# A four-layer graph network on one core: giving each tile the buffer that the plan chose for it

## The chip, the core and the metric

The kernel runs on one core of a Trainium2 chip. A core has TensorE (PE, matrix products and transposes into PSUM), VectorE (DVE), ScalarE (ACT), GpSimd (POOL) and SyncE (SP), which here only issues DMA transfers. Each engine runs its own instructions in the order in which the program gives them. The metric is the time of one execution on the device in microseconds; smaller is better.

## The reference, cut to what matters

There are 64 independent graphs of 256 nodes with 256 features, all in float32. Four graph layers follow each other, each with its own residual and layer norm:

```python
# x, adj: (64, 256, 256)
x = _layernorm(x + L0(x, adj))   # 4 heads: sigmoid(q k^T) * adj, scaled by degree^-1/2 on both sides, times X; layer norm
x = _layernorm(x + L1(x, adj))   # 8 heads: softmax(q k^T where adj > 0), times v, then W_o
x = _layernorm(x + L2(x, adj))   # (adj + eps) x, W1 (256 to 1024), rms norm, silu, W2
x = _layernorm(x + L3(x, adj))   # one-head attention from two scores, softmax, times Wh, layer norm, gelu
```

## The kernel before

**Tiling.** A graph has two blocks of 128 nodes, and a feature axis two blocks of 128. Nearly every tile is 128 partitions by 512 words: both blocks side by side. The function `graph` describes the work of one graph as a list of `Op`s. An Op has an engine, an estimated cost, a function that issues its instructions, and the tiles (`Value`s) that it writes and reads. Nothing is issued while the list is made.

**The order.** `Plan.order` goes through all 64 graphs' Ops at once with a small model of the engines' clocks. Again and again it takes the ready Op that can start soonest, and among equals the one due first. Graphs so overlap: while one is in its last layer, others are in earlier ones. The order that comes out is kept: the framework is told not to reorder (`manual_schedule`), and each engine runs its list front to back. An instruction that must wait holds all that stand behind it on the same engine. Before an ACT function whose table isn't loaded, the build places a table load.

**The buffers.** There are six kinds of tile, each with a fixed number of buffers:

```python
WORDS = {"s": 516, "d": 1024, "b": 2048, "c": 32, "p": 512, "h": 1024}
SLOTS = {"s": 42, "d": 10, "b": 3, "c": 72, "p": 8, "h": 8}
```

Kind `s` is the 512-word tile in SBUF, `p` a bank of PSUM, `c` a few scalars per partition, `h` a scratch area in DRAM. The model also keeps the buffers' books: when a tile is first needed it takes the slot that the model says falls free earliest (`v.slot = self.free[v.kind].pop(0)[1]`), and gives it back at the modelled end of the last use. In the kernel before, `v.slot` serves this reckoning alone. `emit` asks the framework's pool of that kind for a tile, and the pool itself decides which of its 42 (10, 3, ...) buffers that is. The framework adds the waits: the first writer of a tile waits until all who use the buffer's former tile are done.

**The steps that are named below**, by line and by the name of their output in the profile:

- Layer 0: L502 (PE, attention scores), L506 (ACT, sigmoid, `att`), L508 (DVE, times adjacency), L514 (DVE, `added`, sums two halves of `att`), L520 (PE, sums `added` over nodes), L542 (PE, reads `v` and `att`), L553 (DVE).
- Layer 1: L582 (PE, scores), L465 and L470 (DVE and ACT, softmax), L618 (PE, attention times `v1` into `av`), L628 and L631 (SP, the softmax sums out to DRAM and back as `rb`), L635 (DVE, `yT` = `av` times `rb`), then PE's product of `yT` with `w_o` at L379.
- Layer 2: L649 and L661 (PE), L666 and L668 (ACT, squares and `hT`), L673 and L675 (DVE, sums of squares), L680 (PE), L697 (DVE), L699 (ACT, silu), L707 (PE).
- Layer 3: L722 (PE), L731 (PE), L335, L341 and L345 (DVE and SP, a transpose by way of DRAM, giving `xT` and `eT`), L453 and L456 (DVE, `y`), L746 (ACT, gelu in place on `y`).
- Everywhere: L323 (PE transposes), L359 (ACT, copies out of PSUM), L368 and L379 (PE, products with weights), L436 (DVE, `y` = product plus residual), L393, L395, L405, L406 and L416 (DVE and POOL, mean and deviation), L420 (ACT, the normalized tile `x`), L431 (DVE, residual plus a row, `xb`).

Of the kernel before, what the change touches and what calls it, by code (L numbers as in the profile page):

```python
# [9 lines left out]
F32 = mybir.dt.float32  # L10
# [3 lines left out]
P = 128  # L14
# [15 lines left out]
WORDS = {"s": 516, "d": 1024, "b": 2048, "c": 32, "p": 512, "h": 1024}  # L30
# [10 lines left out]
SLOTS = {"s": 42, "d": 10, "b": 3, "c": 72, "p": 8, "h": 8}  # L41
# [710 lines left out]
@with_exitstack  # L752
def gnn_stack_kernel(ctx: ExitStack, tc: tile.TileContext, t: dict, out: bass.AP):

    nc = tc.nc
    x_in, xT_in, adj_in, adjT_in = t["x"], t["xT"], t["adj"], t["adjT"]
    B, N, D = x_in.shape
    NB, DB = N // P, D // P
    assert NB == 2 and DB == 2
    H0, H1 = 4, 8
    HD0, HD1 = D // H0, D // H1
    HID = t["L2_gnn_W1"].shape[1]
    HB = HID // P  # L770

    const = ctx.enter_context(tc.tile_pool(name="const", bufs=1))
    pools = {kind: ctx.enter_context(tc.tile_pool(name=f"pool_{kind}", bufs=SLOTS[kind], **(
        {"space": {"p": bass.MemoryType.PSUM, "h": bass.MemoryType.DRAM}[kind]} if kind in "ph" else {})))
        for kind in SLOTS}


    ident = const.tile([P, P], F32, name="ident")
    make_identity(nc, ident)
    ones = const.tile([P, 32], F32, name="ones")  # L780
    nc.vector.memset(ones, 1.0)
    mean_of = const.tile([P, 32], F32, name="mean_of")
    nc.vector.memset(mean_of, 1.0 / HID)
    mhalf = const.tile([P, 8], F32, name="mhalf")
    nc.vector.memset(mhalf, -0.5)
    c = SimpleNamespace(const=const, ident=ident, ones=ones, mean_of=mean_of, mhalf=mhalf)

    plan = Plan(B)
    weights(plan, nc, c, t)
    for b in range(B):  # L790
        plan.graph = b
        graph(plan, nc, c, t, out, b)
    engines = {mybir.EngineType.PE, mybir.EngineType.DVE, mybir.EngineType.Activation, mybir.EngineType.Pool,
               mybir.EngineType.SP}
    with tc.manual_schedule(engines=engines):
        emit(plan, pools)


def emit(plan, pools):
    for op in plan.order():  # L800
        for v in op.takes:
            v.full = pools[v.kind].tile([P, WORDS[v.kind]], F32, tag=v.kind, name=v.name)
            v.t = v.full[:, :512] if v.kind == "s" else v.full
        op.fn()

# [30 lines left out]
```

## Time and profile before

| | |
|---|---|
| time, median of 3 runs | 2722.47 us (2721.5 to 2724.49) |
| profiled execution, its own time | 2719.01 us |
| its span, first to last instruction | 2717.2 us |
| busy PE, DVE, ACT, POOL | 2669.2, 2438.3, 2231.0, 594.8 us |
| granted TensorE clock | 0.998 of full |
| instructions in the profile | 56606 |

The span is the stretch in which the profile can place work; the 1.8 us between it and the execution's own time lie around it. "Busy" counts the time in which an engine computes, not the time in which it waits. In a list of waits, `A <- B` means that A's engine stood idle before A, and that what came last of the things A needed was B. In the chain of waits, each step is followed back from the last instruction to what released it.

### The profile page before, as it was taken

To read this page: it belongs to the slowest core of one execution; us is meant where nothing else is said; L and a number is where in the kernel's file an instruction comes from. 1 tells how busy PE (TensorE), PEld (TensorE's weight loads), DVE (VectorE), ACT (ScalarE), POOL (GpSimd) and SP (SyncE) were. 2 spreads that over 40 slices of the span, in tenths; PEclk is the share of its full clock that TensorE was granted. 3 is DMA by queue.
4 is the path that set the end of the run, shared out by engine and by line. 5 is a ranking of instruction groups with operands and counts; after the bars stand their busy time and mean duration, and the time that the engine had idled before them with its cause. 6 is when DMAs were issued, how large, how long until landed. Compare 5 with 4: busy or idle time off the path is not lost.

```text
span 2717.2 us, 56606 instructions
## 1 busy us (share of the span) xinstructions
PE 2669.2 (98%) x17568; PEld 2142.3 (79%) x17568; DVE 2438.3 (90%) x7480; ACT 2231.0 (82%) x5343; POOL 594.8 (22%) x902
## 2 busy tenths in 40 slices
PE   8999999999999999999999999999999999999997
PEld 6778787787787877877878777877778788787776
DVE  6888999899899998999989999989999899999986
ACT  4978788887887888878888888888888888888886
POOL 1121222212222222222222222222222222222212
PEclk9999999999999999999999999999999999999999
DMA  5476776776676766767767677676676676766661
GB/s 153 149 205 187 202 205 178 192 205 179 188 193 176 214 186 181 198 172 204 207 161 205 184 189 211 170 190 193 172 215 188 171 212 183 191 210 177 174 169 38
DMA packets 708045, 501.01 MB, mean 184 GB/s; under 512 B 309792, under 2 KB 667552, under 8 KB 707744
## 3 DMA queue, kind: packets, MB, share of 16 engines
q1 hardware_dynamic: 707744, 497.40, 66.5%
q8 instruction: 140, 2.29, 0.4%
q14 instruction: 161, 1.32, 0.2%
HBM read 301.35 MB, written 195.82 MB: 183 GB/s over the span
## 4 chain that ended last, share of the span: by engine, by line
PE 87%; DVE 5%; ACT 3%; DMA 3%; SPq 1%; issue 1%; POOL 0%; DVEq 0%; ACTq 0%; POOLq 0%
PE ps L368 16%; PE ps L379 15%; PE ps L707 14%; PE ps L661 14%; PE ps L582 4%; PE ps L542 4%; PE ps L502 4%; PE ps L722 4%; PE ps L649 4%; PE av L618 4%; DMA eT<-far 1%; PE ps L323 1%; PE ps L520 1%; DVE st L393 1%; ACT e L470 1%
## 5 line engine op out<-in xcount | busy, mean ns | idle before, releaser
L470 ACT ACTIVATE e<-e,low 128x256 f32<-128x256 f32 x1152 | 574.8, 500 | 84.3 <-DVE low L465 83.5
L707 PE MATMUL ps<-w,hT 128*128 128x256 f32 x2048 | 466.8, 380 | 1.3 <-ACT hT L699 1.2
L661 PE MATMUL ps<-aggT,w 128*128 128x256 f32 x2048 | 463.4, 380 | 1.6 <-ACT aggT L359 1.0
L707 PEld LDWEIGHTS ps<-w,hT 128*128 128x128 f32 x2048 | 385.7, 190 | 60.4 <-issue 4.6
L661 PEld LDWEIGHTS ps<-aggT,w 128*128 128x128 f32 x2048 | 383.3, 190 | 57.0 <-issue 2.8
L405 POOL TENSOR_SCALAR mv<-mv 128x2 f32<-128x2 f32 x384 | 132.9, 346 | 1348.3 <-DVE mv L395 966.7
L465 DVE CUSTOM_DVE_ANT_0 e<-ps,adj 128x256 f32<-128x256 f32 x1024 | 361.7, 419 | 25.2 <-PE ps L582 25.1
L406 POOL TENSOR_TENSOR mv<-mv,mhalf 128x2 f32<-128x2 f32 x384 | 307.6, 801 | 32.0
L603 DVE STREAM_TRANSPOSE eb<-e 128x1024 f32<-128x1024 f32 x248 | 301.1, 1222 | 0.8 <-ACT e L470 0.7
L668 ACT ACTIVATE hT<-ps,br,r 128x256 f32<-128x256 f32 x512 | 255.6, 584 | 35.1 <-PE ps L707 31.8
L420 ACT ACTIVATE x<-y,mv 128x256 f32<-128x256 f32 x384 | 215.2, 599 | 55.4 <-DVE mv L416 51.8
L666 ACT ACTIVATE sq<-ps,b 128x256 f32<-128x256 f32 x512 | 219.8, 473 | 27.2 <-PE ps L661 25.0
L393 DVE BATCH_NORM_STATS2 st<-y 128x6 f32<-128x256 f32 x640 | 238.9, 410 | 1.2
L470 ACT ACTIVATION_READ_ACCUMULATOR e<-e,low 128x1 f32 x1152 | 219.4, 190 | 0.0
L508 DVE TENSOR_TENSOR att<-att,adjT 128x512 f32<-128x512 f32 x256 | 166.8, 677 | 7.9 <-ACT att L506 7.9
L688 POOL TENSOR_TENSOR rs<-rs,mhalf 128x2 f32<-128x2 f32 x64 | 45.6, 712 | 526.7 <-DVE rs L686 521.2
L528 POOL TENSOR_TENSOR dp<-dp,mhalf 128x8 f32<-128x8 f32 x64 | 109.7, 1714 | 210.3 <-DVE dp L527 164.4
L697 DVE TENSOR_TENSOR hT<-hT,pr 128x1024 f32<-128x1024 f32 x128 | 150.0, 1210 | 5.2 <-PE pr L693 4.5
L582 PE MATMUL ps<-kT,qT 32*128 32x256 f32 x2048 | 147.5, 400 | 0.0
L673 DVE TENSOR_TENSOR sq<-sq 128x512 f32<-128x512 f32 x192 | 129.9, 677 | 12.1 <-ACT sq L666 11.1
L368 PE MATMUL ps<-x0T,w_q 128*128 128x256 f32 x512 | 130.0, 384 | 6.1 <-DMA x0T<-in_xT 6.1
L506 ACT ACTIVATE att<-ps 128x512 f32<-128x512 f32 x256 | 132.2, 603 | 3.9 <-PE ps L502 3.2
(119 smaller groups left out, 5511.4 us busy)
## 6 DMA issues: line engine op xcount, KB each, us to landing
far<-eb SPq DMA_DIRECT2D x248, 512.0 KB, 3.6
eT<-far SPq DMA_DIRECT2D x992, 128.0 KB, 4.1
adj<-in_adj SPq DMA_DIRECT2D x128, 256.0 KB, 5.0
far<-eb SPq DMA_DIRECT2D x488, 64.0 KB, 2.0
x0T<-in_xT SPq DMA_DIRECT2D x64, 256.0 KB, 4.8
adjT<-in_adjT SPq DMA_DIRECT2D x64, 256.0 KB, 5.0
x<-in_x SPq DMA_DIRECT2D x64, 256.0 KB, 5.2
adj<-in_adjT SPq DMA_DIRECT2D x64, 256.0 KB, 4.6
```

Of the source, the lines that this page charges most:

```text
L368: pe.matmul(two(ps)[:, o, :], w.t[:, k, o * P:(o + 1) * P], two(xT)[:, k, :], start=(k == 0), stop=(k == DB - 1))
L379: pe.matmul(two(ps)[:, n, :], two(xT)[:, k, n * P:(n + 1) * P], w()[:, k, :], start=(k == 0), stop=(k == DB - 1))
L393: op("DVE", 328, lambda n=n: dve.bn_stats(st.t[:, 6 * n:6 * n + 6], two(src)[:, n, :]), [(st, n)], [(src, n)])
L406: pool.tensor_tensor(m()[:, :, 2], m()[:, :, 2], c.mhalf[:, :NB], OP.pow)
L465: op("DVE", 345, lambda n=n: dve.tensor_tensor_reduce(out=E(n), in0=two(logits)[:, n, :], in1=two(negmask)[:, n, :], scale=-scale, scalar= ...
L470: op("ACT", 491, lambda n=n: act.activation(E(n), E(n), AF.Exp, bias=low.t[:, n:n + 1], scale=-1.0, accum_out=r.t[:, col(n):col(n) + 1]), ...
L582: pe.matmul(two(pss[i])[:, n, :], two(qT1)[s, hq, n * P:(n + 1) * P], two(kT1)[s, hq, :], start=True, stop=True)
L603: op("DVE", 1155, lambda e=e, eb=eb: dve.transpose(eb.t.rearrange("p (b g i) -> p g b i", b=4, i=32), e.t.rearrange("p (g b i) -> p g b i" ...
L661: pe.matmul(two(ps)[:, i, :], c.w2_1.t[:, k, (j + i) * P:(j + i + 1) * P], two(aggT)[:, k, :], start=(k == 0), stop=(k == DB - 1))
L666: op("ACT", 357, lambda ps=ps, sq=sq, i=i, j=j: act.activation(two(sq)[:, i, :], two(ps)[:, i, :], AF.Square, bias=c.b2_1.t[:, j + i:j + i ...
L668: op("ACT", 491, lambda ps=ps, i=i, j=j: act.activation(Hb(j + i)[:, 0], two(ps)[:, i, :], AF.Identity, bias=c.br2.t[:, j + i:j + i + 1], ...
L707: pe.matmul(two(ps)[:, n, :], Hb(j)[:, 0, n * P:(n + 1) * P], c.w2_2.t[:, j, :], start=(j == 0), stop=(j == HB - 1))
```

## The change

Each slot gets a pool tag of its own with a single buffer, so `s0`, `s1` and so on up to `h7`. When a tile is taken, the tag is made of its kind and of the slot number that the plan wrote into `v.slot`. So the pool has nothing left to choose: the tile lies where the plan's books say. The numbers of buffers, the sizes, the list of Ops and the plan's model are untouched. The title of the change speaks of "the order in which ACT helps DVE in the last three graphs": that order is set by `ENDS = 3` in `normed` and `affine`, and stands in both kernels.

```diff
-    pools = {kind: ctx.enter_context(tc.tile_pool(name=f"pool_{kind}", bufs=SLOTS[kind], **(
+    pools = {kind: ctx.enter_context(tc.tile_pool(name=f"pool_{kind}", bufs=1, **(
         {"space": {"p": bass.MemoryType.PSUM, "h": bass.MemoryType.DRAM}[kind]} if kind in "ph" else {})))
         for kind in SLOTS}
...
     for op in plan.order():
         for v in op.takes:
-            v.full = pools[v.kind].tile([P, WORDS[v.kind]], F32, tag=v.kind, name=v.name)
+            v.full = pools[v.kind].tile([P, WORDS[v.kind]], F32, tag=f"{v.kind}{v.slot}", name=v.name)
             v.t = v.full[:, :512] if v.kind == "s" else v.full
         op.fn()
```

## The prediction

> **What bounds the kernel now.** I read the page first: shares by engine, then the chain that ended last.
>
> ```profile
> PE 2669.2 (98%) x17568; PEld 2142.3 (79%) x17568; DVE 2438.3 (90%) x7480; ACT 2231.0 (82%) x5343; POOL 594.8 (22%) x902
> ...
> PE 87%; DVE 5%; ACT 3%; DMA 3%; SPq 1%; issue 1%; POOL 0%; DVEq 0%; ACTq 0%; POOLq 0%
> ```
>
> TensorE is busy 98% of 2717.2 us and makes up 87% of the chain. Nothing in the change shortens a matmul, so all that can be won is TensorE's idle time, 2717.2 - 2669.2 = 48 us, of which some belongs to start and end. Next, the waits of PE, from 300 to 2250 us, where the graphs follow each other in a steady pattern:
>
> ```profile
> PE ps L323 <- ACT x L420: 5.6, 10, 1.0
> PE ps L379 <- DVE mv L395: 2.9, 10, 0.4
> PE ps L323 <- DVE y L436: 2.3, 5, 0.5
> PE ps L520 <- DVE added L514: 2.2, 5, 0.4
> ```
>
> The columns are total us, times, longest. All come 5 or 10 times: the pattern repeats every 334 us (eight graphs), five times in this stretch. (The line "mv L395" is really the yT multiply L635, which ends 0.1 us earlier; L379 reads yT.) What are those DVE and ACT results late for? The waits of DVE over the whole span:
>
> ```profile
> DVE y L436 <- PE av L618: 11.2, 9, 1.6
> ...
> DVE added L514 <- PE ps L379: 9.5, 5, 1.9
> DVE yT L635 <- PE ps L542: 9.1, 7, 1.6
> ...
> DVE added L514 <- PE ps L542: 5.8, 5, 1.2
> ```
>
> By the code these are strange. L514 adds two att halves and needs nothing from L379 or L542; L436 needs neither av nor L618; L635 needs av (L618), not L542. So these 35.6 us are waits for a **buffer**: the output was given a buffer whose former tile (v0, yT, v1) TensorE was still reading. The chain shows that this reaches the end:
>
> ```profile
> 693.92 0.66 PE ps L379 x3
> ...
> 694.60 0.69 DVE added L514
> 695.30 0.33 DVE sq L675
> 695.63 0.08 DVE mv L416
> ...
> 695.74 1.10 ACT x L420 x2
> ...
> 696.89 0.55 PE ps L323 x3
> ```
>
> DVE stands still until L379 has read yT. Behind L514 in DVE's queue are L675 and L416, for L416 ACT's L420 waits, for that TensorE's L323. TensorE waits for itself, round a loop that data do not ask for.
>
> **What the Trainium skill says.** "Perfetto Trace Analysis", Optimization Strategy: the same gap repeating on the engine that should be saturated can mean that there is no buffer for the next tile. The trace agrees (5 times each at 334 us); here the buffers exist, and the wrong one is taken. The same page, Identifying Dependency Chains: an instruction that waits for several engines may get EventSemaphore instructions ahead of it. The trace shows 732 on PE. "ScalarE: Activation LUTs", What ACT_TABLE_LOAD costs: 1283 ns, with a drain some 2.66 us. Here each load takes 1283 ns, and the sigmoid below starts 0.02 us after its load; that drain is not seen.
>
> **The change, part by part.** Built, both programs have the same instructions in the same order on all five queues, SP's and POOL's included; no DMA is added or moved. Only addresses differ, and with them what is waited for. So I laid the waits of the changed program on the times of this trace: when was each new releaser done, against when its waiter started?
>
> 1. *Waits for buffers that go.* The plan's slot is the one that it reckons free earliest. For the 512-word SBUF buffers, re-uses within 2 us of the former tile's last use fall from 170 to 103 of 2704. On DVE 30 stalls end sooner, 40 us in sum, on ACT 9 for 6 us, on PE itself 0.6 us. Most of that is cover, as TensorE wasn't waiting. What counts, per 334 us:
>  - 696 us: L514 may go when L673 is done, 692.86 instead of 694.58: 1.7 us. L416 and L420 come 1.7 us earlier, and both halves of L323 lose their stalls, 0.96 and 0.16 us idle.
>  - 531 us: the second L514 goes at 528.8 instead of 530.0; L520 loses 0.44, and L379 0.40, since L635 follows L514 on DVE.
>  - 611 us: L436 goes at 608.8 instead of 610.4; L323 loses 0.47. L635 then waits for its data alone (L618, 610.35), ends near 611.0 instead of 612.7, and L379 loses 0.18.
>  Sum of idle: 2.6 us. A matmul's record runs 0.17 us past the start of the next in full flow (four L379 records at 0.216 us apart last 1.03 us), so each of the six stalls costs 0.17 more: 2.6 + 1.0 = 3.6 us, five times: **18.0 us**. Near the end ACT's L666 waits at 2455.8 for a DMA out of its buffer (1.84 us); behind it are L673, L675 and PE's L680, idle 1.1 us at 2462: **1.1 us**. Together 19.1 us.
> 2. *Waits that are new and late.* On PE, DVE and POOL none: the tightest new one on PE is done 0.04 us before it is needed. On SP's queue four: an rb load (L631) at 289 us by 1.95 us, and eT loads (L345) by 0.81, 0.29 and 0.15, each with later DMAs queued behind it. eT and rb feed TensorE, so I charge all 3.2 us, although the three eT waits are for L436 near the 696 us place, which itself comes earlier.
> 3. *Table loads.* Gelu gets a second wait (its buffer), so one wait moves to an EventSemaphore, and that stands ahead of the table load:
>
> ```profile
> 512.43 1.28 ACT L746 ACT_TABLE_LOAD   x1
> 514.14 0.63 ACT L746 ACTIVATE y<-y 128x512 f32<-128x512 f32 x1 [0.43 <-DVE y L456]
> 514.79 1.28 ACT L506 ACT_TABLE_LOAD   x1
> 516.09 0.60 ACT L506 ACTIVATE att<-ps 128x512 f32<-128x512 f32 x1
> ```
>
>  Today the load runs while L456 is computed. Changed, 11 of the 61 Gelu loads wait for L456: two delay Gelu by the full 1.28, six by 0.92, three by 0.50: 9.6 us on ACT. Queued behind are L506, L666 and L668. The first matmuls that need these (L731 at 518.93, L661 at 519.15) have 2.2 and 2.0 us in hand; at 428 us none has under 2.5. I cost this at nothing on the path; ACT idles 18% and catches up. Without that cover it is 9.6 us.
> 4. *EventSemaphores:* PE 732 to 683, ACT 971 to 941, DVE 972 to 948, SP 1182 to 1177, POOL 288 to 289. Where the wait is met early they take no engine time: L680 to L582 is 156 ns with or without one. Nothing.
> 5. *Addresses:* no row shows a cost of place. L514 takes 641 to 695 ns over its 128 runs through rotating buffers. I take nothing; bound 1 us either way.
>
> Sum: 3.2 - 19.1 = -15.9 us. Against the profiled execution, 2719.0 (span 2717.2 and 1.8 around it), 2703.1. The median of the runs is 3.5 us above that execution, so 2722.5 - 15.9 = **2706.6 us**.
>
> **The rivals.**
> - *The stalls move on.* TensorE comes early and waits at the next join instead, such as L722 for the xT DMA (0.3 us idle at 461.8, met in most repeats; the waits name ACT L470, done long before). For it: several joins have 0.3 to 0.9 us in hand. Against: those are chains that TensorE itself starts a few us before, which move with it, and DVE loses more idle time (40 us) than PE. Half the gain left: 2714.5; a tenth: 2721.
> - *Slower, by table loads.* Ten more Gelu loads lie within 0.25 us of being late, as DVE and ACT shift. If 21 loads cost ACT 1.28 us each and TensorE waits for all of it, +26.9 - 15.9 = +11.0: 2733.5. It decides from 12.4 full loads reaching TensorE (15.9 / 1.28). Against: the 2 us in hand above, and an earlier DVE makes L456 earlier too.
> - *The change doesn't do what its title says.* It names ACT helping DVE in the last three graphs. No instruction changes its engine or place, so nothing comes from that. If the pool's choice was as good as the plan's, no change: 2722.5. The 35.6 us of waits that data do not ask for speak against it.
> - *More than counted.* DVE's other gains also fill PE's remaining waits (for L699, L359, L675): another 6 to 8 us, 2699.
>
> **How the numbers follow.** About 0.2% (5.4 us) is what a measurement can tell from no change. The forecast gets 0.67 (its own range 2700 to 2712), more than counted 0.05, stalls partly moved on 0.10: faster 0.82. A gain under 5.4 us, or none, 0.13. Slower by table loads 0.05. The range 2698 to 2719 takes in the charge for DMA left away (-3), the added gain, and half or less of the gain; it leaves out most of no change and the slower case.
>
> **What would show it.** Right: DVE's waits of L514 for L379 and L542 and of L436 for L618 are gone; PE's waits at L323 and L520 fall under 2 us in all; DVE idles less before them; the chain has less DVE than 5%. ACT shows longer waits at L746's table load for L456. Wrong: PE's waits sum to some 30 us as now under other names, above all DMA (L722, L379 with eT) or ACT (L506, L668 after a Gelu load); then the stalls have moved.

## The result: 0.991 of the time before

The changed kernel takes 2699.1 us (2695.65 to 2700.52, six runs) against 2722.8 us (2721.5 to 2726.04, six runs of the kernel before on the same chip). The ratio is 0.9909, with a 95% interval from 0.9896 to 0.9921: 23.7 us less by the medians, where 15.9 us were forecast. The new time lies in the range of 2698 to 2719 us, near its low end, and just below the 2700 to 2712 us that the forecast called its own.

**The profile after.** First the page: the shares by engine, then the chain that ended last.

```profile
PE 2666.0 (99%) x17568; PEld 2144.9 (79%) x17568; DVE 2436.7 (90%) x7480; ACT 2228.8 (83%) x5343; POOL 588.5 (22%) x902
...
PE 93%; DVE 3%; ACT 2%; DMA 1%; SPq 1%; issue 1%; POOL 0%; ACTq 0%; POOLq 0%; DVEq 0%
```

The work is the same: DVE and ACT are busy within 2.2 us of before. What has changed is the chain: TensorE makes up 93% of it instead of 87%, DVE 3% instead of 5%. Now the waits of PE in the changed kernel, from 300 to 2250 us. This is the whole answer:

```profile
PE ps L722 <- DVE hT L697: 0.6, 2, 0.4
```

The four rows of before (13.0 us in 30 waits) are gone, and no other wait has taken their place. Of DVE's waits, those of L514 for L379 and L542, of L436 for L618 and of L635 for L542 are gone too. What is left at these lines, over the whole span of the changed kernel, is this:

```profile
DVE yT L635 <- PE av L618: 19.8, 16, 2.5
...
DVE y L436 <- PE ps L379: 11.0, 14, 1.7
...
DVE y L436 <- PE ps L707: 6.0, 8, 1.6
```

All three are waits for data: L635 multiplies `av`, which L618 makes, and L436 adds to a product that L379 or L707 makes. The loop at 696 us is broken. Below are the same instructions in the timeline of the changed kernel (start, duration, engine, line; a bracket at the end would be idle time before the instruction):

```profile
692.07 0.68 DVE L514 TENSOR_TENSOR added<-att 128x512 f32<-128x512 f32 x1
692.14 1.89 PE L379 MATMUL ps<-w_o,yT 128*128 128x256 f32 x8
...
693.01 0.15 DVE L416 SCALAR_TENSOR_TENSOR mv<-mv 128x2 f32<-128x2 f32 x1
...
693.26 1.09 ACT L420 ACTIVATE x<-y,mv 128x256 f32<-128x256 f32 x2
...
693.87 1.03 PE L379 MATMUL ps<-w_l,x0T 128*128 128x256 f32 x4
...
694.74 0.60 PE L323 MATMUL ps<-ident,x 128*128 128x128 f32 x4
```

L514 now starts before the product of yT does, instead of after its end. L420 is done before L323's turn comes, and L323 follows L379 without a bracket: its four matmuls are one piece, where there were two stalls.

**Why 18.6 us in the profiled pair and 23.7 us in the medians?** The spans of the two profiled executions are 2717.2 and 2698.6 us. Their TensorE clock isn't equal. The view of a stretch gives the window, its length, busy us and records of PE, PEld, DVE, ACT and POOL, then the granted clock, the DMA share and GB/s. The changed kernel first:

```profile
65.00:73.00 8.00, 6.58 (x18) 5.20 (x17) 3.95 (x15) 5.78 (x19) 1.87 (x4) 0.57 0.50 156
```

The kernel before:

```profile
65.00:73.00 8.00, 7.68 (x48) 6.51 (x49) 2.95 (x13) 7.98 (x23) 0.93 (x2) 1.00 0.40 130
```

The profiled execution of the changed kernel had 0.57 of the clock in these 8 us, and the window holds 18 matmul records against 48, though not all of them the same matmuls. Matched matmul by matmul, from start to start, the first 100 us cost it 3.8 us more than the kernel before, all in L368 at half speed: 2.9 us here, and 0.8 us near 9 us, where its clock rose to full 2.1 us later. By the mean clock not all executions have this: of the six runs, three have spans of 2693.9, 2694.1 and 2695.9 us at 0.998, and three of 2698.6 to 2698.7 us at 0.997. The kernel before, in the 17 runs beside the first experiments, has 13 between 2717.7 and 2720.7 us at 0.998. At like clock the two are some 24 us apart.

### The profile page after: what moved, and what is told of

Same layout as the page of the kernel before. It is cut to its first block, busy times and chain, and to the rows that moved or that the text cites. A ratio compares the mean times of both kernels' runs of the same rounds, so it can differ in the third digit from the quotient of the medians.

```text
span 2698.6 us, 56499 instructions
## 1 busy us (share of the span) xinstructions
PE 2666.0 (99%) x17568; PEld 2144.9 (79%) x17568; DVE 2436.7 (90%) x7480; ACT 2228.8 (83%) x5343; POOL 588.5 (22%) x902
## 4 chain that ended last, share of the span: by engine, by line
PE 93%; DVE 3%; ACT 2%; DMA 1%; SPq 1%; issue 1%; POOL 0%; ACTq 0%; POOLq 0%; DVEq 0%
PE ps L368 16%; PE ps L707 16%; PE ps L661 16%; PE ps L379 15%; PE ps L582 5%; PE ps L502 4%; PE ps L542 4%; PE av L618 4%; PE ps L722 4%; PE ps L649 4%; PE ps L323 1%; PE ps L520 1%; PE pr L693 1%; DVE e L465 1%; PE ps L731 0%
## 5 line engine op out<-in xcount | busy, mean ns | idle before, releaser
L707 PE MATMUL ps<-w,hT 128*128 128x256 f32 x2048 | 466.8, 380 | 1.3 <-ACT hT L699 1.2
L707 PEld LDWEIGHTS ps<-w,hT 128*128 128x128 f32 x2048 | 385.7, 190 | 60.4 <-issue 4.6
L420 ACT ACTIVATE x<-y,mv 128x256 f32<-128x256 f32 x384 | 215.2, 600 | 28.9 <-DVE mv L416 26.1
L508 DVE TENSOR_TENSOR att<-att,adjT 128x512 f32<-128x512 f32 x256 | 166.4, 676 | 10.0 <-ACT att L506 10.0
L582 PE MATMUL ps<-kT,qT 32*128 32x256 f32 x2048 | 146.2, 399 | 0.0
L673 DVE TENSOR_TENSOR sq<-sq 128x512 f32<-128x512 f32 x192 | 129.5, 675 | 11.1 <-ACT sq L666 10.2
L368 PE MATMUL ps<-x0T,w_q 128*128 128x256 f32 x512 | 130.4, 385 | 6.6 <-DMA x0T<-in_xT 6.6
```

The lines of the kernel that those rows point to most:

```text
L368: pe.matmul(two(ps)[:, o, :], w.t[:, k, o * P:(o + 1) * P], two(xT)[:, k, :], start=(k == 0), stop=(k == DB - 1))
L582: pe.matmul(two(pss[i])[:, n, :], two(qT1)[s, hq, n * P:(n + 1) * P], two(kT1)[s, hq, :], start=True, stop=True)
L707: pe.matmul(two(ps)[:, n, :], Hb(j)[:, 0, n * P:(n + 1) * P], c.w2_2.t[:, j, :], start=(j == 0), stop=(j == HB - 1))
```

## The experiments

Theory A is that of the prediction: DVE's outputs were given 512-word SBUF buffers (kind `s`) that TensorE was still reading, and at a few places this came back to TensorE. Theory B: it was the PSUM banks. Theory C: there are fewer separate wait instructions. Theory D: it takes the plan's own assignment, not just a buffer that is free. Apart from the separate wait instructions, all kernels have the instructions of the kernel before, in the same order on every engine. Differences are between medians, against the kernel before on the same chip, with the interval of the ratio.

### The changed kernel again

> The changed kernel once more, as the yardstick of this chip. Theory A (the pool gave DVE outputs the wrong 512-word SBUF buffer, kind s): 19 us less than before, as in the profiled pair, up to the 24 us between the medians. If the 5 us between these two figures come from the TensorE clock early in an execution, single runs fall in two groups some 5 us apart.

Measured: 2699.94 us against 2721.43, -21.5 us; ratio 0.992 (0.9906 to 0.9934). The spans are 2694.2 us at a clock of 0.998, 2697.9 and 2698.1 at 0.997, 2699.9 and 2700.2 at 0.996: the time follows the clock, though in three groups, not two.

### One half of the change: kind `s` alone

```diff
-... bufs=SLOTS[kind], **(
+... bufs=1 if kind == "s" else SLOTS[kind], **(
...
-            v.full = pools[v.kind].tile(..., tag=v.kind, name=v.name)
+            v.full = pools[v.kind].tile(..., tag=f"s{v.slot}" if v.kind == "s" else v.kind, name=v.name)
```

> Only kind s is named by the plan's slots; PSUM, scalars, the 1024- and 2048-word tiles and DRAM stay with the pool. Theory A: nearly the whole gain, 16 to 20 us less than before; laid on the trace of the changed kernel, PE has 4.2 us of late waits, six of them L379 for ACT L627. Theory B (PSUM banks were the wrong ones): under 5 us. Theory C (fewer separate wait instructions): about half, 10 us, since 29 of the 49 removed on PE go.

Measured: 2703.01 us, -18.4 us; ratio 0.9929 (0.9916 to 0.9941). PE's waits from 300 to 2250 us show what is missing to the full change:

```profile
PE ps L379 <- ACT rT L627: 2.3, 6, 0.4
PE ps L722 <- DMA xT<-far: 0.3, 1, 0.3
```

The six waits of L379 for L627 are there as expected: 2.3 us idle, and at 0.17 us each for a matmul's fill some 3.3 us, where the medians of the two kernels differ by 3.1. L379 reads nothing that L627 makes: it is a PSUM bank that the pool chose. The clock blurs this comparison: four of these five runs had 0.998 of it, with spans of 2698.7 to 2701.8 us, and only one of the changed kernel's five did, with 2694.2. At like clock the two may lie some 5 us apart. So kind `s` brings most of the gain, and naming the other kinds adds a few us on top of it.

### The other half: all kinds but `s`

```diff
-... bufs=SLOTS[kind], **(
+... bufs=SLOTS[kind] if kind == "s" else 1, **(
...
-            v.full = pools[v.kind].tile(..., tag=v.kind, name=v.name)
+            v.full = pools[v.kind].tile(..., tag="s" if v.kind == "s" else f"{v.kind}{v.slot}", name=v.name)
```

> The complement: all kinds but s are named. Theory A: 0 to 4 us less than before, with DVE's waits of L514 for L379 and L542 and of L436 for L618 as before. Theory B: 15 us or more. Theory C: about 10 us, 37 separate waits on PE go.

Measured: 2721.57 us, +0.1 us; ratio 1.0 (0.9992 to 1.0008). PE's waits over the same stretch:

```profile
PE ps L323 <- ACT x L420: 5.6, 10, 1.0
PE ps L379 <- DVE mv L395: 2.9, 10, 0.4
PE ps L323 <- DVE y L436: 2.3, 5, 0.5
PE ps L520 <- DVE added L514: 2.2, 5, 0.4
```

These are, digit for digit, the four rows of the kernel before. DVE's waits of L436 for L618 (11.9 us), of L514 for L379 (9.2) and of L514 for L542 (5.8) are there as before, too. Theories B and C fall as the cause of the gain: 37 of the 49 separate wait instructions that the change takes from PE are gone here too, and nothing is won.

### The pool still chooses, from two more buffers

```diff
-... bufs=SLOTS[kind], **(
+... bufs=SLOTS[kind] + 2 * (kind == "s"), **(
```

> The kernel before, the pool still choosing, but its kind s has 44 buffers where the plan counts 42. Theory A: the pool can avoid a buffer that is still being read, so 14 to 20 us less than before. If the gain needs the plan's own assignment (theory D), under 6 us. Laid on the trace of the changed kernel, DVE has 3 us of late waits left of 51.

Measured: 2699.36 us, -22.1 us; ratio 0.992 (0.9906 to 0.9933). Two spare buffers to the 42 do about what the plan's own names do, and theory D falls. L323 keeps a trace of the old stall:

```profile
PE ps L323 <- ACT x L420: 0.8, 5, 0.2
PE ps L722 <- DMA xT<-far: 0.7, 1, 0.7
```

### L514's output in two buffers of its own

```diff
+    pools["own"] = ctx.enter_context(tc.tile_pool(name="pool_own", bufs=2))
...
+            own = v.name == "added"
-            v.full = pools[v.kind].tile(..., tag=v.kind, name=v.name)
+            v.full = pools["own" if own else v.kind].tile(..., tag="own" if own else v.kind, name=v.name)
```

> The kernel before, but the tiles named added (L514) have two buffers of their own and no longer take one of the pool's 42. Theory A with its prices: the stalls at 696 us (1.5 us) and at 531 us (1.2 us) go, five times each, the one at 611 us (0.9 us, L436) may stay: 13 to 18 us less than before. If the gain comes from elsewhere: under 5 us.

Measured: 2700.35 us, -22.3 us; ratio 0.9915 (0.9901 to 0.9928). More than expected, since the place at 611 us is mended too: with `added` out of the pool, L436 got a better buffer there as well, and one row is all that PE waits from 300 to 2250 us:

```profile
PE ps L722 <- PE ps L649: 0.4, 2, 0.2
```

Taking one kind of output out of the pool moves the choice for all the others, and it makes 44 buffers in all, as in the experiment before. So this isn't a clean price of L514 alone.

### The output of L436 in two buffers of its own

```diff
...
+        y.from_plus = True          # in plus(), L436
...
+    pools["own"] = ctx.enter_context(tc.tile_pool(name="pool_own", bufs=2))
...
+            own = v.name == "y" and v.from_plus
```

> The kernel before, but the tiles y of L436 have two buffers of their own. Theory A: the stall at 611 us goes (0.9 us, five times), L514 still waits for L379 at 696 us (1.5 us, five times); what becomes of the 531 us place is open: 4 to 11 us less than before, with L323 still waiting for ACT L420 five times. If only the sum of DVE's idle time counts and not its place, 12 us or more, since 28 of the 51 us of late waits on DVE go.

Measured: 2712.57 us, -10.1 us; ratio 0.9957 (0.9945 to 0.997). Here are the waits of PE from 300 to 2250 us, and below them one of DVE's over the whole span (lines behind the 435th are one higher in this kernel, so L514 is L515):

```profile
PE ps L323 <- ACT x L420: 5.6, 10, 1.0
PE ps L379 <- DMA eT<-far: 1.8, 1, 1.8
PE ps L723 <- DMA xT<-far: 1.4, 3, 0.5
```

```profile
DVE added L515 <- PE ps L379: 9.2, 5, 1.9
```

L436's own row and that of L520 are gone; the loop at 696 us stands, ten waits of PE and five of DVE as before. This kernel has 44 buffers of 512 words too, and comes out at half the gain, so it isn't their number alone that counts. This is the half-way kernel: it loses 5.6 us idle and 1.7 us of fill (ten times 0.17) at that one place, and it comes out 12.2 us behind the kernel that freed L514; the two DMA rows, and 1.8 us at L680 near the end, make up the rest. That the place of a wait counts, and not the sum of DVE's idle time, is shown by these ten waits rather than by the time. By the reckoning made ahead of the run, 28 of DVE's 51 us of late waits were to go, and by the sum alone that was to give 12 us or more; the interval of the ratio, 8.2 to 15.0 us, doesn't exclude it.

### The buffer that fell free last

```diff
+PICK = lambda free, op: max((i for i in range(len(free)) if free[i][0] <= op.start), key=lambda i: free[i], ...)
-    for op in plan.order():
+    for op in reslot(plan.order(), PICK):        # new slots of kind s, the order kept
```

> The changed kernel, same order, but each tile of kind s takes the buffer that fell free last by the plan's clock, not first. Laid on the trace of the changed kernel, no wait on PE is late; ACT has 19 us of late waits, SP 10, DVE 4. Theory A (what counts is whether TensorE waits in the end): 0 to 8 us more than the changed kernel, still faster than before. If any late wait costs its full length: 30 us more, slower than before.

Measured: 2698.16 us, -24.5 us; ratio 0.9909 (0.9895 to 0.9922). It is as good as the changed kernel; PE's longest row from 300 to 2250 us is 0.8 us at L722. So the plan's rule, earliest first, isn't what helps: taking last what falls free first does as well, as long as the plan's clock counts the buffer as free. The late waits that were expected on ACT and SP, 29 us by their lengths, cost nothing that shows. Two of those on ACT can be seen by name in its waits over the whole span, which the changed kernel doesn't have:

```profile
ACT aggT L359 <- DVE y L456: 10.3, 4, 2.6
...
ACT xT L359 <- DVE att L508: 5.1, 7, 0.8
```

L359 copies what TensorE left in PSUM and reads nothing of L456 or L508, so these 15.4 us are waits for room.

### The buffer released first in program order

```diff
+PICK = lambda free, op: 0
```

> The changed kernel, same order, but each tile of kind s takes the buffer that was released first in program order, whatever the plan's clock says of it. 28 us of late waits on DVE, nearly all for a DMA that still reads the buffer (L628, L749, L341), in queues ahead of L514 and L436. Theory A: these sit at the same DVE steps as those of the kernel before, so TensorE stalls again: 5 to 15 us more than the changed kernel. If such waits are covered: 0 to 3 us more.

Measured: 2712.59 us, -10.0 us; ratio 0.9965 (0.9952 to 0.9977), 14.4 us behind the kernel of the last experiment on the same chip. The waits of PE from 300 to 2250 us, and below them two of DVE's over the whole span:

```profile
PE ps L323 <- DVE y L436: 3.5, 5, 1.0
PE ps L323 <- ACT x L420: 1.5, 6, 0.6
PE ps L379 <- DVE yT L635: 1.4, 1, 1.4
PE ps L379 <- DVE mv L395: 0.8, 5, 0.2
```

```profile
DVE added L514 <- DMA out<-o: 5.7, 5, 1.9
...
DVE y L436 <- DMA far<-rT: 3.5, 2, 2.2
```

L514 and L436 now wait for a DMA that still reads the buffer, and the same joins of TensorE come late again. Order in the program is a poor guess of order in time where DMAs end late. It isn't what the pool did either: the late waits of L514 were for TensorE there, and are for DMA here. By what rule the pool chose stays open.

## Why the prediction was right, point by point

- **What bounds the kernel.** Right: TensorE's waits behind DVE. With them gone, PE is 99% busy, and nothing else came forward.
- **Step 1, the three places.** Right in size. From start to start of the same matmuls in the two profiles, the six stalls gave back 7.55, 5.89 and 4.39 us in five repeats (696, 531 and 611 us): 17.8 us, where 18.0 were forecast. L680 near the end gave 1.05 us (1.1). The idle time alone, 13 us, would have been too little; the 4.8 us between it and 17.8 are 0.16 us for each of the 30 stalls, so the 0.17 us of fill belongs to it.
- **Step 1, what wasn't counted.** The waits that go were followed only where the pattern repeats and near the end. Between 200 and 300 us, where the graphs are still being staggered, TensorE gained another 3.5 us: 0.7 at L693, 0.9 at L379 for yT, the rest at L582. The first two, 0.7 and 1.0 us, were won as well with all kinds but `s` named, so they can't be put down to kind `s`; what they hang on is open. The rival "more than counted" had the direction and, with 2699 us, the figure, but not the mechanism. It named PE's waits for L699, L359 and L675, and those for L699 (1.2 us) and L359 (1.6, 1.4, 1.0 and 1.0 us) are the same in both kernels; only that for L675 went, and step 1 had counted it. The stretch from 100 to 200 us gave 0.9 us back, at L520 and L582.
- **Step 2, new late waits on SP, 3.2 us.** The term that was mis-sized: it was zero. PE's waits name no `rb`, and no `eT` from 300 to 2250 us. The three eT waits were for L436 beside the 696 us place, which itself came earlier, as the prediction noted and then charged all the same. The rb wait may have been real: L631 was issued at 292.4 us instead of 288.8, of which 2.9 us are TensorE's own delay at that place, from the later start and the slower clock ahead of it. TensorE gained in that stretch all the same.
- **Step 3, table loads.** Right that they cost nothing on the path. In the changed kernel the Gelu loads wait like this (timeline of ACT, at the place shown before):

```profile
514.08 1.28 ACT L746 ACT_TABLE_LOAD   x1 [0.58 <-DVE y L456]
515.37 0.63 ACT L746 ACTIVATE y<-y 128x512 f32<-128x512 f32 x1
```

  The load starts only when L456 is done, as forecast. Gelu comes at 515.37 instead of 514.14, but ACT's copy just ahead (L359, `aggT`) stands at 512.92 instead of 511.83, 1.1 us later as well: L456 came earlier by most of the load, and Gelu is delayed by only 0.14 us against the rest. Elsewhere it is more. Twelve of the 61 loads wait, one of them in both kernels; the other 11 are what was forecast, and measured against TensorE's own shift they put Gelu off by 10.3 us in all (9.6 forecast), by 1.74 us at most. Yet TensorE doesn't wait for ACT once between 300 and 2250 us. The slower rival needed 12.4 full loads to reach TensorE; none did.
- **Steps 4 and 5, wait instructions and addresses.** Nothing that shows, as forecast: naming all kinds but `s` takes away 37 wait instructions on PE for +0.1 us, and giving the tiles of kind `s` other buffers, last instead of first, leaves the time as it was.
- **The sum.** In the profiled pair, 17.8 + 1.05 + 3.5, and 0.7 at L722 and 0.7 elsewhere, make 23.7 us of stalls won (only by chance the figure of the medians too); 0.9 lost at 100 us and 3.8 lost to the half clock leave 19.0 us between the first and the last matmul. That 15.9 came near 18.6 is thus in part chance: 3.2 us charged for nothing, and a clock that no step had in it. Without both, the steps make 19.1 us against 22.8 at like clock, and what is missing is for the most part the 3.5 us between 200 and 300 us. The medians, at 23.7 us, are half as much again as was forecast.
- **The rival that the stalls move on** is out: 0.6 us of waits are left from 300 to 2250 us, where half the gain lost would have left some 6.5 of the 13 us under other names.

## What to carry to other kernels

Where an engine waits for another whose result it doesn't read, look for the former tile of its output buffer: a wait for room looks like a wait for data, and stands in front of all that is queued behind it. A plan that keeps books of buffers should also place the tiles, or the pool should have a few to spare: two more on top of 42 were worth about as much here. And price such waits by what the saturated engine does next: 15.4 us of them on ACT, with the buffer that fell free last, cost nothing that shows, while 9.5 us on DVE ahead of one join cost 7.6.

## What the runs showed of the hardware

**Separate wait instructions on PE.** With 37 of 732 fewer, the time moved by 0.1 us, with an interval of some 2 us either way.

**A second wait ahead of a table load.** In the changed kernel it stands ahead of the load, so that the 1283 ns load no longer runs under the wait. Eleven of 61 Gelus came later for it, by 0.14 to 1.74 us, and nothing came of that on TensorE.

**Half the clock.** In five of the ten profiled executions the TensorE clock fell to half near 66 us: three times for 3.41 us, twice for 6.83 us. It cost 2.9 us in the changed kernel's profile. Each time it fell 54.61 us after the clock had first risen to full, and 54.61 and 6.83 are 16 and 2 times 3.413; the full stretches of the other profiles are whole multiples of it, too. The stalls of PE just ahead (0.30, 0.65 and 1.42 us within 5 us) are the same in all ten, so they don't decide it alone. What differs is when the clock first rose: at 11.1 us or later in these five, at 10.9 us or earlier in the others. The kernel with all kinds but `s` named had half the clock once more, for 3.41 us near 2464 us, behind a stall of 2.4 us. What sets it off stays open.
